# Moving the statistics of one norm, one tile of another, and the buffer of the recurrence's first input

## The chip, the core and the metric

The kernel runs on one core of a Trainium2 chip. A core has five engines that run their own instruction streams and wait for each other through semaphores: TensorE (PE in the profile, its weight loads PEld), VectorE (DVE), ScalarE (ACT), GpSimd (POOL) and SyncE (SP), which here issues nearly all DMAs. The metric is the device time of one execution in microseconds (us), as a median over runs.

## The reference, cut to what matters

Two layers act on 2 sequences of 1024 tokens with 512 channels. The kernel cuts the 2048 tokens into four blocks of 512 (b = 0 to 3).

```python
x = L0_attn_hidden_states
x = _layernorm(x + _L0_attn_ref(x, ...))   # mamba: in-projection, causal conv, scan, gate, RMS norm, out-projection
x = _layernorm(x + _L0_ffn_ref(x, ...))    # one linear layer, rows scaled by a tanh of their norm
x = _layernorm(x + _L1_attn_ref(x, ...))   # gated linear recurrence: conv, two gates, scan, out-projection
x = _layernorm(x + _L1_ffn_ref(x, ...))    # gated FFN of 512 -> 2048 -> 512 with integer weights

def _layernorm(x, axis=-1, eps=1e-05):
    m = jnp.mean(x, axis=axis, keepdims=True)
    v = jnp.var(x, axis=axis, keepdims=True)
    return (x - m) / jnp.sqrt(v + eps)
```

## The kernel before

**Who sets the order.** Python generators interleave the stages of neighbouring blocks: the order in which instructions are traced. A scheduler then orders each engine's stream by priority (earlier traced first) among what is ready in its own simulation. Three things bind it: `manual_schedule` for the opening, `high_priority` (not used at the places of this change before it), and `keep_in_program_order(ins)`, which pins an instruction behind the instruction of its engine that was traced just before it. That orders issue only; it is no wait for data.

**First layer, by block.** `project(b)` makes eight convolved channel tiles `inner(m)`: four matmuls `px` (L366), copies by ScalarE (L508, L336), three taps on VectorE (`causal_conv`, L292) and a SiLU (L342). Woven in are the decay products: ScalarE copies rows of `L` into PSUM (`pl`, L566), VectorE scans them (L572), GpSimd multiplies them (L587). `fill`, the generator `conclude(b - 1)`, puts the output projection of the block before (`po`, L764, and the residual update on VectorE, L779) between them, by `plan = (0, 0, 2, 0, 2, 0, 2, 2)`: eight steps, which are all the steps up to the last residual update. What follows in `conclude`, `layernorm(X[b])` and `store_rows(x_mid[b], X[b])`, is traced in the ninth step, which `weave` takes inside `recur(b)`, after the instructions of its first chunk of 128 tokens (`py` L691 and L699, `pst` L709, updates of the state L716 and L723, `by_token` L668 and L670).

**`layernorm`** (L274) makes per tile of 128 rows `bn_stats` (L279) and `bn_aggr` (L280) on VectorE, one square root on ScalarE (L282), one reciprocal (L283) and four scalings (L285) on VectorE or on the engine given.

**`head(b + 1)`** follows in the same alternation: for blocks 2 and 3 it turns the input with four VectorE transposes (`turn_blocks`, L270), each pinned; the first one is therefore queued behind the last scaling of the norm just traced. TensorE then makes `pbc` (L387) from it, from which the decays of the next block come.

**Second layer and recurrence.** `later_layers` weaves `conclude(3)` with `linear(0)` and `linear(1)`. Each `linear(b)` transposes its input on TensorE (`pt`, L237), splits it into two parts (`wu` by ScalarE L241, `wd` by VectorE L244), multiplies (`po`, L968), and ends with a norm whose four scalings run on GpSimd. Then `branches(0)` transposes X[0] (L237), ScalarE copies the result to `xT` (L248), and the products `p` (L1050) read it. `xT` of block 0 lies in pool `rp`, tag "xT"; that pool is on the right side, which the first layer's tiles used till then. The input of `linear(3)`, `mid`, lies in pool `wp`, tag "w4", and is loaded from `x_mid[3]`, which `conclude(3)` stores; the tag "w4" later takes the recurrence's output weights. In `rp`, tag "xT" serves `xT` of blocks 1 to 3 afterwards.

Of the kernel before, what the change touches and what calls it, by code (L numbers as in the profile page):

```python
# [9 lines left out]
F32 = mybir.dt.float32  # L10
# [6 lines left out]
P = 128  # L17
TB = 512
NJ = TB // P
D = 512  # L20
NK = D // P
# [16 lines left out]
def model_kernel(ctx: ExitStack, tc: tile.TileContext, t: dict, out: bass.AP):  # L38
    nc = tc.nc
# [6 lines left out]
    x_mid = tc.dram_tile([NBLK, TB, D], F32, name="x_mid")  # L46
# [35 lines left out]
    X = [tokens() for _ in range(3)]  # L82
# [140 lines left out]
        nc.vector.tensor_scalar(r, z, 0.0, None, ALU.max)  # L223
        nc.vector.scalar_tensor_tensor(o, p, 2.0, r, ALU.mult, ALU.add)

    def transposed(pool, b, X, tags=("xT",), split=False, bufs=1, by_act=False, behind=False):


        pieces = [
            pool.tile([P, NK, TB], F32R if split else F32, tag=tag, name=f"{tag}{b}", bufs=bufs)  # L230
            for tag in tags
        ]
        xT = pieces[0]
        for k in range(NK):
            pt = bank("pt")
            for j in range(NJ):
                nc.tensor.transpose(  # L237
                    pt[:, j * P : (j + 1) * P], X[b][:, j, k * P : (k + 1) * P], ident
                )
            if split:  # L240
                copied = nc.scalar.copy(xT[:, k, :], pt)  # L241
                if behind:
                    tc.keep_in_program_order(copied)
                nc.vector.tensor_tensor(  # L244
                    pieces[1][:, k, :], pt, xT[:, k, :].bitcast(F32), ALU.subtract
                )
            elif k % 2 or by_act:
                nc.scalar.copy(xT[:, k, :], pt)  # L248
            else:
                nc.vector.tensor_copy(xT[:, k, :], pt)  # L250
        return pieces
# [6 lines left out]
    def load_blocks(dst, rows, pinned=False):  # L258

        blocks = rows.rearrange("(n t) (k a c) -> a t k n c", t=32, k=NK, c=32)  # L260
        for a in range(4):
            load = nc.sync.dma_start(
                dst[32 * a : 32 * a + 32].rearrange("t k (n c) -> t k n c", c=32), blocks[a]
            )
            if pinned:
                tc.keep_in_program_order(load)
# [4 lines left out]
            if pinned:  # L271
                tc.keep_in_program_order(turned)

    def layernorm(x, n=NJ, engine=nc.vector):  # L274

        mv = sp.tile([P, NJ, 2], F32, tag="mv", name="mv")
        for j in range(n):
            st = sp.tile([P, 6], F32, tag="st", name="st", bufs=4)
            nc.vector.bn_stats(st, x[:, j, :])  # L279
            nc.vector.bn_aggr(mv[:, j, :], st)  # L280
        rs = sp.tile([P, NJ, 1], F32, tag="rs", name="rs")
        nc.scalar.activation(rs[:, :n], mv[:, :n, 1:2], AF.Sqrt, bias=eps)  # L282
        nc.vector.reciprocal(rs[:, :n], rs[:, :n])  # L283
        for j in range(n):
            engine.tensor_scalar(  # L285
                x[:, j, :], x[:, j, :], mv[:, j, 0:1], rs[:, j, :], ALU.subtract, ALU.mult
            )

# [467 lines left out]
    def conclude(b, st):  # L756


        xc, sums = st["xc"], st["sums"]
        rms = sp.tile([P, NJ], F32, tag="rms", name="rms")  # L760
        for j in range(NJ):
            po = bank("po")
            for m in range(NX):
                nc.tensor.matmul(  # L764
                    po, xc[:, m, j * P : (j + 1) * P], w_out[:, m, :],
                    start=(m == 0), stop=(m == NX - 1),
                )
                if m == NX // 2 - 1:
                    yield
            if j == 0:  # L770
                pss = bank("pss")
                for i in range(NJ):
                    nc.tensor.matmul(
                        pss[:, i : i + 1], sums[:, i * P : (i + 1) * P], ones,
                        start=True, stop=True,
                    )
                nc.scalar.activation(rms, pss[:, :NJ], AF.Sqrt, bias=eps, scale=1.0 / DI)
                nc.vector.reciprocal(rms, rms)
            nc.vector.scalar_tensor_tensor(  # L779
                X[b][:, j, :], po, rms[:, j : j + 1], X[b][:, j, :], ALU.mult, ALU.add  # L780
            )
            yield
        layernorm(X[b])
        store_rows(x_mid[b], X[b])

    def by_blocks(b, st):
# [4 lines left out]
    H, before, st = None, None, {}  # L791
# [10 lines left out]
    for b in range(NBLK):  # L802
# [19 lines left out]
        before, st = st, coming  # L822
    before_last.close()
    last = (conclude(NBLK - 1, before), first_layer.close)
# [41 lines left out]
    def later_layers(exact, last=None):  # L866


        suffix = "" if exact else "g"
        WT = F32R if exact else F32  # L870
        X = Y
# [4 lines left out]
        wp = opened.enter_context(tc.tile_pool(name="w" + suffix, bufs=1, reuse_waits="tile"))  # L876
# [72 lines left out]
        def linear(b):  # L949

            tags = ("wu0", "wd0") if exact else ("wu0",)
            if b == NBLK - 1:
                turn_blocks(mid)
                w1.append(wp.tile([P, NK, D], F32, tag="w4", name="w14" + suffix))
                xT = [ep.tile([P, NK, TB], WT, tag=tag, name=f"{tag}{b}") for tag in tags]
                split(mid, xT)
                nc.sync.dma_start(w1[4], w_sources["w_out"])
            else:

                xT = transposed(ep, b, X, tags=tags, split=exact, behind=b == 2)  # L960
            yield
            o = ep.tile([P, NJ, D], F32, tag="wF", name="o" + suffix)
            ssq = sp.tile([P, NJ], F32, tag="ssq", name="ssq")
            for j in range(NJ):
                po = bank("po")
                for k in range(NK):
                    for x in xT:
                        nc.tensor.matmul(  # L968
                            po, x[:, k, j * P : (j + 1) * P], wf[:, k, :],
                            start=(k == 0 and x is xT[0]), stop=(k == NK - 1 and x is xT[-1]),  # L970
                        )
                nc.vector.tensor_tensor(o[:, j, :], po, f0s, ALU.mult)
                junk = ep.tile([P, GW], mybir.dt.bfloat16, tag="junk", name="junk2")
                nc.scalar.activation(junk, o[:, j, :], AF.Square, accum_out=ssq[:, j : j + 1])
                if j % 2:
                    yield
            norm = sp.tile([P, NJ], F32, tag="norm", name="norm")
            nc.scalar.activation(norm, ssq, AF.Sqrt)
            v = sp.tile([P, NJ], F32, tag="v", name="v")
            nc.vector.tensor_scalar(v, norm, 1e-7, None, ALU.max)  # L980
            f = sp.tile([P, NJ], F32, tag="f", name="f")
            nc.scalar.activation(f, v, AF.Tanh)
            nc.vector.tensor_scalar(v, v, 1e-7, None, ALU.add)
            nc.vector.reciprocal(v, v)
            nc.vector.tensor_tensor(f, f, v, ALU.mult)
            nc.vector.tensor_tensor(norm, norm, f, ALU.mult)
            nc.vector.tensor_scalar(norm, norm, 1e-7, None, ALU.max)
            nc.vector.reciprocal(norm, norm)
            nc.vector.tensor_scalar(norm, norm, 0.99, 1.0, ALU.mult, ALU.min)
            nc.vector.tensor_tensor(f, f, norm, ALU.mult)  # L990
            for j in range(NJ):
                nc.vector.scalar_tensor_tensor(
                    X[b][:, j, :], o[:, j, :], f[:, j : j + 1], X[b][:, j, :],
                    ALU.mult, ALU.add,
                )
            layernorm(X[b], engine=nc.gpsimd)
            if b:
                store_rows(x_lin[b], X[b])
            yield
# [8 lines left out]
                pass  # L1008
        for i, name in ((2, "w_ig"), (3, "w_ag")):
            nc.sync.dma_start(w1[i], w_sources[name])  # L1010

        mid = wp.tile([P, NK, TB], F32, tag="w4", name="mid" + suffix)
        load_blocks(mid, x_mid[3])
        nc.sync.dma_start(X[3], rows_mid[3])

        def gate_up(m):

# [25 lines left out]
        with tc.tile_pool(name="rec" + suffix, bufs=1, side="right", reuse_waits="tile") as rp:  # L1043
            carry = rp.tile([P, NK, 3], F32, tag="carry", name="carry1")
            last_h = rp.tile([P, NK], F32, tag="last", name="last")

            def product(i, m, rhs):
                pm = bank("p1")
                for k in range(NK):
                    nc.tensor.matmul(  # L1050
                        pm, w1[i][:, k, m * P : (m + 1) * P], rhs[:, k, :],
                        start=(k == 0), stop=(k == NK - 1),
                    )
                return pm

            def branches(b, st):

                if b:
                    xT = rp.tile([P, NK, TB], F32, tag="xT", name=f"xT{b}")
                    turn_blocks(xT, lin.pop(0))  # L1060
                    if b + 1 < NBLK:
                        lin.append(coming_block(b + 1))
                else:
                    xT = transposed(rp, b, X, by_act=True)[0]
                yield
                cv = st["cv"] = rp.tile([P, NK, TB], F32, tag="cv", name="cv", bufs=2)
                y = st["y"] = rp.tile([P, NK, TB], F32, tag="y", name="y", bufs=2)
# [98 lines left out]
            st = {}  # L1166
# [260 lines left out]
```

## Time and profile before

| what | us |
|---|---|
| median of 3 runs (1121.63 to 1123.01) | 1121.71 |
| profiled execution, whole time | 1122.32 |
| its span, first to last instruction | 1120.5 |
| stretch of block 1's projection, from its third `px` pair to the first token transposes | 119.08 to 161.34 |
| the same stretch of block 2 | 226.49 to 264.33 |

The page gives busy time by engine, a row of busy tenths over 40 slices, the costliest groups and the chain of work that ended last. Further views are the waits of one engine (who was waited for, total us, how often, longest), the timeline of one engine (start, length, line, tile, count, and in brackets the idle time before it with what ended it), and tables of stretches (busy us and instructions of each engine, granted TensorE clock as a share of full speed, DMA share, GB/s). Times in all of them count from the start of the span.

### The profile page before, as it was taken

The numbers are of one execution on the slowest core, as the hardware profiler recorded it, in microseconds if no ns is written. First come the engines' busy times: TensorE is split into PE (matmuls) and PEld (weight loads), VectorE is DVE, ScalarE is ACT, GpSimd is POOL, SyncE is SP. The second block draws the span as 40 slices with busy tenths as digits, with TensorE's granted clock in tenths as the row PEclk, the third lists the DMA queues.
The fourth block names the chain that finished last, engine by engine and source line by source line (L and its number), as shares of the span: only waits on it lengthen the run. The fifth ranks groups of instructions, "written<-read, shape, count | busy, mean of one in ns | idle before, by whom it ended". The sixth has DMA issues, their size and how long they took to land.

```text
span 1120.5 us, 12075 instructions
## 1 busy us (share of the span) xinstructions
PE 1102.6 (98%) x4450; PEld 664.5 (59%) x4450; DVE 704.6 (63%) x1266; ACT 453.6 (40%) x692; POOL 366.5 (33%) x347
## 2 busy tenths in 40 slices
PE   9999999999999999999999999999999999999996
PEld 5455445445544555645444444447888888888885
DVE  5989897697869676874646438184238865325224
ACT  3334633463454233556644372553223224224223
POOL 1547471465248340453433231236411001001000
PEclk9999999999999999999999999999999999999999
DMA  9005302801220138246540001304654002100001
GB/s 325 19 11 119 95 1 92 206 1 38 82 105 0 39 125 224 57 103 151 112 76 8 30 1 38 38 0 130 193 100 75 1 1 59 17 1 29 9 1 41
DMA packets 122059, 77.04 MB, mean 69 GB/s; under 512 B 94512, under 2 KB 95312, under 8 KB 120456
## 3 DMA queue, kind: packets, MB, share of 16 engines
q1 hardware_dynamic: 120792, 75.77, 25.9%
q8 instruction: 37, 0.61, 0.2%
q10 hardware_dynamic: 976, 0.39, 0.1%
q14 instruction: 30, 0.25, 0.1%
q0 software_dynamic: 224, 0.02, 0.0%
HBM read 59.95 MB, written 16.02 MB: 68 GB/s over the span
## 4 chain that ended last, share of the span: by engine, by line
PE 82%; DVE 10%; ACT 4%; issue 1%; POOL 1%; DMA 1%; SPq 0%; DVEq 0%; ACTq 0%; POOLq 0%
PE pgu L1024 20%; PE p L1050 19%; PE po L1250 10%; PE pg L366 9%; PE px L366 7%; PE po L764 6%; PE po L1139 2%; PE py L699 2%; PE po L968 2%; DVE L L572 2%; DVE acc L292 2%; PE pxt L668 1%; POOL x L1145 1%; DVE st L279 1%; PE pbc L387 1%
## 5 line engine op out<-in xcount | busy, mean ns | idle before, releaser
L1035 DVE SCALAR_TENSOR_TENSOR h<-pgu,L_ffn_up_scale,sg 128x512 f32<-128x512 f32 x63 | 47.1, 748 | 126.5 <-PE pgu L1024 122.7
L764 PE MATMUL po<-w_out,xc 128*128 128x512 f32 x256 | 114.2, 600 | 2.2 <-DVE L L572 2.2
L366 PE MATMUL px<-xT,w_in 128*128 128x512 f32 x256 | 114.6, 597 | 0.0
L587 POOL TENSOR_TENSOR L<-L,gm 128x512 f32<-128x512 f32 x64 | 93.0, 1483 | 64.8 <-DVE bdec L582 38.3
L366 PE MATMUL pg<-xT,w_in 128*128 128x512 f32 x256 | 113.5, 594 | 0.0
L1050 PE MATMUL p<-xT,w 128*128 128x512 f32 x256 | 111.1, 592 | 1.0 <-ACT xT L248 1.0
L1050 PE MATMUL p<-cv,w 128*128 128x512 f32 x256 | 110.8, 592 | 0.0
L1024 PE MATMUL pgu<-wF__4239,wg 128*128 128x512 f32 x256 | 101.7, 397 | 0.0
L1024 PE MATMUL pgu<-lo__4240,wg 128*128 128x512 f32 x256 | 100.8, 394 | 0.0
L1024 PE MATMUL pgu<-lo__4240,wu 128*128 128x512 f32 x256 | 100.7, 393 | 0.0
L1024 PE MATMUL pgu<-wF__4239,wu 128*128 128x512 f32 x256 | 100.7, 393 | 0.0
L1250 PE MATMUL po<-wd,hh 128*128 128x512 f32 x252 | 98.3, 396 | 0.3 <-POOL wg L911 0.3
L1250 PE MATMUL po<-wd,hl 128*128 128x512 f32 x252 | 98.2, 396 | 0.2 <-DVE hl L1039 0.2
L1034 ACT ACTIVATE sg<-pgu,L_ffn_gate_scale 128x512 f32<-128x512 f32 x63 | 43.4, 689 | 125.6 <-PE pgu L1024 125.5
L764 PEld LDWEIGHTS po<-w_out,xc 128*128 128x128 f32 x256 | 49.0, 192 | 64.3 <-issue 57.1
L1038 ACT CAST hh<-h 128x512 fp32r<-128x512 f32 x63 | 39.1, 621 | 114.6 <-DVE h L1035 114.4
L1050 PEld LDWEIGHTS p<-xT,w 128*128 128x128 f32 x256 | 48.5, 190 | 60.8 <-issue 57.6
L1050 PEld LDWEIGHTS p<-cv,w 128*128 128x128 f32 x256 | 48.6, 190 | 60.4 <-issue 59.1
L366 PEld LDWEIGHTS px<-xT,w_in 128*128 128x128 f32 x256 | 47.5, 190 | 57.5 <-issue 56.2
L366 PEld LDWEIGHTS pg<-xT,w_in 128*128 128x128 f32 x256 | 47.3, 190 | 54.2 <-issue 53.3
L292 DVE SCALAR_TENSOR_TENSOR acc<-xpad,cols,acc 128x512 f32<-128x512 f32 x72 | 67.2, 935 | 18.9 <-ACT acc L336 14.1
L1368 POOL TENSOR_TENSOR x<-x,r 128x512 f32<-128x512 f32 x12 | 15.2, 1300 | 194.2 <-DVE r L1367 194.2
(291 smaller groups left out, 1929.2 us busy)
## 6 DMA issues: line engine op xcount, KB each, us to landing
L<-decays SPq DMA_DIRECT2D x12, 1024.0 KB, 7.1
x_mid<-x SPq DMA_DIRECT2D x4, 1024.0 KB, 4.3
x<-x_mid SPq DMA_DIRECT2D x4, 1024.0 KB, 8.1
st<-in_L_ffn_gate_w_dram SPq DMA_DIRECT2D x8, 512.0 KB
st<-in_L_ffn_up_w_dram SPq DMA_DIRECT2D x8, 512.0 KB, 3.9
st<-in_L_ffn_down_w_dram SPq DMA_DIRECT2D x8, 512.0 KB, 4.1
x_rec<-x SPq DMA_DIRECT2D x4, 1024.0 KB, 4.7
x<-_attn_hidden_states_dram SPq DMA_DIRECT2D x3, 1024.0 KB
```

The source lines that it names most:

```text
L292: tap = nc.vector.scalar_tensor_tensor(acc, xpad[:, k : k + TB], w[:, k : k + 1], acc, ALU.mult, ALU.add)
L366: nc.tensor.matmul(pm[:n, :], w_in[:, k, lo : lo + n], xT[:, k, :], start=(k == 0), stop=(k == NK - 1),)
L572: nc.vector.tensor_tensor_scan(L[:, h, :], pl, id4.rearrange("p j t -> p (j t)"), 0.0, ALU.mult, ALU.add)
L587: nc.gpsimd.tensor_tensor(L[:, h, :], L[:, h, :], st["gm"], ALU.mult)
L699: nc.tensor.matmul(pys[i][hh * HD : (hh + 1) * HD, q, :], dtx[q][:, 2 * i + hh, :], L[:, h, s], start=(first and q == 0), stop=(q == 1), s ...
L764: nc.tensor.matmul(po, xc[:, m, j * P : (j + 1) * P], w_out[:, m, :], start=(m == 0), stop=(m == NX - 1),)
L1024: nc.tensor.matmul(pm, w[g][:, k, cols], x[:, k, :], start=(k == 0 and x is pieces[0]), stop=(k == NK - 1 and x is pieces[-1]),)
L1034: nc.scalar.activation(sg, pgu[0], AF.Silu, scale=gs[:, m : m + 1])
L1035: nc.vector.scalar_tensor_tensor(h, pgu[1], us[:, m : m + 1], sg, ALU.mult, ALU.mult)
L1038: nc.scalar.copy(halves[0], h)
L1050: nc.tensor.matmul(pm, w1[i][:, k, m * P : (m + 1) * P], rhs[:, k, :], start=(k == 0), stop=(k == NK - 1),)
L1250: nc.tensor.matmul(po[j], x[:, j * P : (j + 1) * P], wd[m // GK][:, m % GK, :], start=(m == 0 and x is h[0]), stop=(m == NF - 1 and x is h ...
```

## The change

Four edits:

- The norm in `conclude(0)` pins each `bn_stats` behind the VectorE instruction traced before it. For the first it is the last product of `by_token` in the first chunk of `recur(1)`; for the others the `bn_aggr` of the tile before.
- In `linear(0)`'s norm the fourth scaling runs on VectorE, the other three stay on GpSimd.
- `xT` of block 0 goes to pool `wp`, tag "w4", and its four ScalarE copies get high priority.
- `mid` goes to pool `rp`, tag "xT"; its four loads and the load of X[3] are traced after that pool is opened.

```diff
-    def transposed(pool, b, X, tags=("xT",), split=False, bufs=1, by_act=False, behind=False):
+    def transposed(pool, b, X, tags=("xT",), split=False, bufs=1, by_act=False, behind=False, soon=False):
...
+            elif soon:
+                with tc.high_priority():
+                    nc.scalar.copy(xT[:, k, :], pt)
             elif k % 2 or by_act:
                 nc.scalar.copy(xT[:, k, :], pt)
...
-    def layernorm(x, n=NJ, engine=nc.vector):
+    def layernorm(x, n=NJ, engine=nc.vector, last=None, pinned=False):
...
-            nc.vector.bn_stats(st, x[:, j, :])
+            stats = nc.vector.bn_stats(st, x[:, j, :])
+            if pinned:
+                tc.keep_in_program_order(stats)
             nc.vector.bn_aggr(mv[:, j, :], st)
...
-            engine.tensor_scalar(
+            (last if last and j == n - 1 else engine).tensor_scalar(
                 x[:, j, :], x[:, j, :], mv[:, j, 0:1], rs[:, j, :], ALU.subtract, ALU.mult
             )
...
-        layernorm(X[b])
+        layernorm(X[b], pinned=b == 0)
         store_rows(x_mid[b], X[b])
...
-            layernorm(X[b], engine=nc.gpsimd)
+            layernorm(X[b], engine=nc.gpsimd, last=None if b else nc.vector)
...
-        mid = wp.tile([P, NK, TB], F32, tag="w4", name="mid" + suffix)
-        load_blocks(mid, x_mid[3])
-        nc.sync.dma_start(X[3], rows_mid[3])
...
+            mid = rp.tile([P, NK, TB], F32, tag="xT", name="mid" + suffix)
+            load_blocks(mid, x_mid[3])
+            nc.sync.dma_start(X[3], rows_mid[3])
...
-                    xT = transposed(rp, b, X, by_act=True)[0]
+                    xT = transposed(wp, b, X, tags=("w4",), by_act=True, soon=True)[0]
```

## The prediction

> **What bounds the kernel now.** First the page's busy row and the waits of TensorE, by quarters of the span.
>
> ```profile
> PE 1102.6 (98%) x4450; PEld 664.5 (59%) x4450; DVE 704.6 (63%) x1266; ACT 453.6 (40%) x692; POOL 366.5 (33%) x347
> PE po L764 <- DVE L L572: 2.2, 2, 1.9
> PE p L1050 <- ACT xT L248: 1.0, 1, 1.0
> PE pt L237 <- POOL xpad L1072: 0.4, 1, 0.4
> ```
>
> TensorE bounds the kernel. It is idle for 17.9 us in all; about 8.4 of that is the tail, about 2 the start. So an edit pays only where it closes a hole of TensorE or shortens its matmuls. The three waits shown are the holes beside which the four edits lie. From 464 us to the FFN's end the stretches show TensorE busy throughout but for 0.5 us, so time won before it arrives at the end.
>
> Next the table of stretches (columns: busy us and count of PE, PEld, DVE, ACT, POOL; clock; DMA share; GB/s), block 1 above block 2:
>
> ```profile
> 133.39:142.37 8.98, 7.03 (x17) 2.85 (x15) 8.88 (x14) 6.11 (x12) 8.32 (x8) 1.00 0.00 0
> 142.37:151.04 8.67, 8.67 (x17) 3.74 (x17) 8.64 (x11) 1.62 (x3) 7.07 (x5) 0.80 0.00 0
> ...
> 240.30:247.17 6.87, 6.87 (x18) 3.04 (x16) 6.84 (x11) 5.97 (x11) 5.85 (x7) 1.00 0.00 0
> 247.17:254.03 6.86, 6.86 (x17) 3.04 (x16) 6.86 (x10) 1.34 (x3) 6.54 (x7) 1.00 0.00 0
> ```
>
> Sixteen matmuls take 6.87 us in block 2. In block 1 the first sixteen are followed by a hole of 1.95, and the next sixteen take 8.67 at a mean clock of 0.80: the two-us windows show the clock at 0.50 from 144 to 146. The whole stretch is 42.26 us (119.08 to 161.34) against 37.84 (226.49 to 264.33) for the same matmuls: 4.42 us are to be had at most.
>
> What VectorE does ahead of the hole:
>
> ```profile
> 136.47 0.70 DVE L279 BATCH_NORM_STATS2 st<-x 128x6 f32<-128x512 f32 x1
> 137.21 0.18 DVE L280 BATCH_NORM_AGGREGATE mv<-st 128x2 f32<-128x6 f32 x1
> 137.31 0.72 DVE L779 SCALAR_TENSOR_TENSOR x<-po,rms,x 128x512 f32<-128x512 f32 x1
> 138.06 0.69 DVE L279 BATCH_NORM_STATS2 st<-x 128x6 f32<-128x512 f32 x1
> 138.79 0.18 DVE L280 BATCH_NORM_AGGREGATE mv<-st 128x2 f32<-128x6 f32 x1
> 138.88 4.55 DVE L572 TENSOR_TENSOR_SCAN L<-pl,id 128x512 f32<-128x512 f32 x4
> 142.37 8.83 PE L764 MATMUL po<-w_out,xc 128*128 128x512 f32 x16 [1.95 <-DVE L L572]
> ```
>
> Two pairs of statistics stand before the scans whose end frees TensorE. In block 2 only one pair stands there, and TensorE does not wait.
>
> **Statistics: what goes.** The pin puts all four pairs behind the first chunk of `recur(1)`. Before the scans that frees 0.82 + 0.85 (the chain's pieces) = 1.67 us. The scans can't use all of it: ScalarE's copies `pl` start at 136.80 and take 0.53 each, so the first scan can start at 137.37 instead of 138.88: 1.51. The hole shrinks from 1.95 to 0.44. What is late next is VectorE. Its sixth convolution ends at 152.2 instead of 153.7. The seventh then waits for ScalarE's SiLU and two copies; block 2 shows 1.93 between the same two convolutions (258.37 to 260.30), so it starts at 154.1 instead of 156.10 and, at its own 4.3, ends at 158.4. Before, VectorE then idled 1.15 for `po`; TensorE, at 119.08 + 37.84 + 0.23 + 0.44 = 157.6, is now there first. The residual update (0.67) follows at once, and the token products (L670) start at 159.1 to 159.3 instead of 162.21. Gain 3.0; bounds 1.5 (the hole alone) and 4.4 (the stretch of block 2).
>
> [...] The row shows half clock behind a hole of only 1.95, and none behind 1.03 at 463. [...] By the row they go with the hole: 3.0. I take the row.
>
> **Statistics: what comes.** Behind 159.3 VectorE keeps its work without the pair at 163.4 and ends the second chunk's token products near 166 (before 169.37, with that pair, the reciprocal and one scaling among them). Then four pairs of 0.85 (3.4), the root (0.4 with its hand-over), the reciprocal (0.2) and four scalings (1.92 in block 2): 171.8. The transposes of block 2's input are pinned behind the last scaling:
>
> ```profile
> 169.29 1.45 DVE L285 TENSOR_SCALAR x<-x,mv,rs 128x512 f32<-128x512 f32 x3
> 170.65 2.48 DVE L270 STREAM_TRANSPOSE xT<-xT 128x512 f32<-128x512 f32 x4
> 177.37 1.51 DVE L292 SCALAR_TENSOR_TENSOR acc<-rpad,cwr,acc 32x512 f32<-32x512 f32 x2 [4.24 <-ACT acc L336]
> ```
>
> They run 171.8 to 174.3, while TensorE, 3.0 earlier, is ready for `pbc` at 170.7. `pbc` would wait; but the scheduler takes the next ready instruction, and the second chunk's `py`, `pst`, `pxt` (4.1 us) are ready by then. I cost this at nothing, with them as cover; without the cover it is rival B. What hangs on `pbc` has room: the decay rows are issued at 192.92 and their loads at 199.30, the first scan of block 2 comes at 225.72. VectorE's 4.24 idle at 177 takes up the rest. The store of `x_mid[0]` moves with the norm on SP's queue; the reload is at 411.
>
> **Second place: `xT`, `mid`, one tile.** ScalarE's, GpSimd's and SP's timelines:
>
> ```profile
> 463.27 2.05 ACT L248 COPY xT<-pt 128x512 f32<-128x512 f32 x4 [0.48 <-DMA x_mid<-x]
> ...
> 451.02 8.42 POOL L285 TENSOR_SCALAR x<-x,mv,rs 128x512 f32<-128x512 f32 x4 [32.70 <-PE pt L237]
> ...
> 458.89 0.37 SPq L254 DMA_DIRECT2D x_mid<-x  x1
> ```
>
> The copies wait for the store of X[3], because `xT` takes the place of a tile that this store reads. In "w4" nothing of that kind stands; the transposes start at 458.6, ScalarE is free, and high priority puts the copies (0.59) ahead of the squares. TensorE's 1.03 goes. `mid` needs that store anyway, as its data; its loads stay behind it on SP (two at 463.21, two at 482.06 behind the store of `x_lin`), and VectorE turns it at 494.87. The next `xT` then waits for `mid`'s last reader (500.2) instead of the products at 498.8, but is turned only at 529.50. The output weights, now behind `xT`, were issued at 518.18 and used at 589. All covered.
>
> The 0.42 is the wait for the fourth tile on GpSimd (2.1 us a tile, end 459.44; the wait row names the memset right behind it). With it on VectorE the third ends at 457.3 and the hole goes. VectorE pays one scaling: 0.54 alone, 0.68 beside GpSimd at 455.50, 1.51 at worst (a row at 756). If it lands before `wd` (L244, 451.34), for which TensorE already waits 0.15 at 452.07, up to 0.6 comes back. [...] By the row at 455.50 it is slowed by 0.14. I take the row. This place: 0.85 to 1.45, taken as 1.2.
>
> **Sum.** 3.0 + 1.2 = 4.2. From the profiled 1122.32 (span 1120.5 and 1.8 around it) to 1118.1; that execution lies 0.6 above the median, so from 1121.71 to **1117.5**, with its own range 1116.0 to 1119.0. A measurement of this kernel can tell 0.2% (2.2 us) from no change.
>
> **Rivals.** *B, the wait moves.* `pbc` keeps its place in TensorE's order and waits for the late transposes: it ends at 174.8 instead of 172.6, 2.2 lost, 1119.7. For: in all blocks `pbc` stands behind two gate tiles. Against: the scheduler sees VectorE's queue. *C, slower.* The same wait, decided by the root: if ScalarE has it behind the second gate tile's SiLU (170.7 + 0.6, a table load of 1.28, 0.3), scalings and transposes end at 177.5 and `pbc` at 178.0: 5.4 lost, and a hole of that size brings the half clock, 1.8 more. 7.2 against 4.2: 1124.7. It decides once the wait at `pbc` exceeds 2.4 (with the clock). Against: in blocks 1 and 2 the root stands before the gates' SiLU (164.34, 270.74). *D, the change does not do what it says.* Another early-ready VectorE instruction takes the freed place before the scans, or a bank is late, and 0.5 is won in block 1: with 1.2, 1120.0.
>
> **Chances.** Forecast 0.57, B 0.16, C 0.15, D 0.12. Faster takes the forecast and half of B: 0.65; same the other half and D: 0.20; slower C: 0.15. The range runs from 1115.7 (4.42 + 1.6) to 1122.5, which holds the forecast, B and D and leaves C out.
>
> **What would show it.** Right: no `bn_stats` between 120 and 163, the stretch near 39 us, clock 1.00 in it, the waits of `po` on L572 below 0.7, `p` not waiting on `xT`. Wrong: a wait of `pbc` on L270, a dip of the clock near 171, a longer wait of `po` L968 on `wd`, or decay loads of block 2 landing late.

## The result, and the profile after

| | median, us | range | executions |
|---|---|---|---|
| before | 1121.81 | 1120.89 to 1123.49 | 22 |
| changed | 1124.39 | 1121.33 to 1125.01 | 22 |

The ratio is 1.0014, with a 95% interval of 1.0008 to 1.002: 0.14% slower where 0.37% faster was forecast. (The two medians alone give 1.0023; they depend on how many executions of each group below they hold.) That is less than the 0.2% which the prediction had set as the bound of a change, and the median lies outside its range of 1115.7 to 1122.5.

The times of the changed kernel fall into groups: five executions lie between 1121.33 and 1121.66, fourteen between 1124.29 and 1125.01, three between them. Those of before do the same: twelve between 1120.89 and 1121.90, ten between 1122.84 and 1123.49. The profiled execution of the changed kernel (1121.35, span 1119.5) is one of its lower five; that of before (1122.32) had the half clock (0.50) in 144 to 146. Two further profiles of the changed kernel caught its upper group (1124.85 and 1124.70); the first of them, with a span of 1123.1, is shown. Both groups are needed to see where the time went.

First the page's busy row and the waits of TensorE in the changed kernel (columns as before: total us, how often, longest).

```profile
PE 1100.4 (98%) x4450; PEld 663.8 (59%) x4450; DVE 704.2 (63%) x1267; ACT 452.7 (40%) x692; POOL 364.2 (33%) x346
...
PE pbc L393 <- issue: 2.0, 1, 2.0
PE po L770 <- DVE L L578: 1.3, 2, 0.8
PE po L974 <- DVE wd L244: 0.8, 1, 0.8
```

The old waits are gone or smaller: `po` on the scans (now L578) is at 1.3 instead of 2.2, and neither the wait on `xT` nor the one on GpSimd is left. Two have come: `pbc` for 2.0, and `po` on `wd` at 0.8 instead of 0.15. (A third, `pt` on the load of the first input, 1.0 near 7 us, differs between profiles of one kernel, and the stretch of block 1 begins within 0.2 us of before in all of them.) The row names "issue" for `pbc`, a wait for nothing that the profile shows. The timelines tell what it was. TensorE, changed kernel:

```profile
127.08 7.13 PE L770 MATMUL po<-w_out,xc 128*128 128x512 f32 x16 [0.83 <-DVE L L578]
...
141.58 7.13 PE L770 MATMUL po<-w_out,xc 128*128 128x512 f32 x16 [0.49 <-DVE L L578]
...
164.35 7.03 PE L372 MATMUL pg<-xT,w_in 128*128 128x512 f32 x16
173.41 0.64 PE L393 MATMUL pbc<-xT,w_bc 128*48 128x256 f32 x4 [2.02 <-issue]
173.97 0.48 PE L697 MATMUL py<-cdec,H 32*128 32x128 f32 x2
174.39 0.64 PE L393 MATMUL pbc<-xT,w_bc 128*48 128x256 f32 x4
174.96 0.48 PE L697 MATMUL py<-cdec,H 32*128 32x128 f32 x2
175.37 1.07 PE L393 MATMUL pbc<-xT,w_bc 128*48 128x256 f32 x8
```

VectorE, changed kernel, the last two rows ahead of `pbc`:

```profile
170.77 1.91 DVE L291 TENSOR_SCALAR x<-x,mv,rs 128x512 f32<-128x512 f32 x4
172.60 2.48 DVE L273 STREAM_TRANSPOSE xT<-xT 128x512 f32<-128x512 f32 x4
```

The hole at which the pin was aimed is nearly closed, 0.49 for 1.95. The one before the scans ahead of it is 0.83, for 0.23 in before. That is no work of the change: another profile of the changed kernel (the one of its second run, below) has 0.49 and 0.23 there.

```profile
PE po L770 <- DVE L L578: 0.7, 2, 0.5
```

So executions of one kernel differ by 0.6 at this place, and the two profiles compared here happen to differ in it; why is not shown. Further on, TensorE stands still from 171.4 and starts `pbc` when the first of the four transposes is done; the products come in three pieces, with a few `py` of the next chunk between them. From the start of the gate tiles `pg` to the second group of the next chunk's `py` (those that read `L`) the time is 12.66 us (164.35 to 177.01); before it was 9.49 (166.72 to 176.21). 3.17 us are given back here.

The starts of the same instructions in three profiles, and the difference from before:

| start of | before | changed, lower group | changed, upper group |
|---|---|---|---|
| first token transposes `pxt`, block 1 | 161.34 | 158.85 (-2.49) | 158.98 (-2.36) |
| gate tiles `pg` behind the first chunk | 166.72 | 164.35 (-2.37) | 164.48 (-2.24) |
| `py` (with `L`) of the second chunk | 176.21 | 177.01 (+0.80) | 179.60 (+3.39) |
| gate tiles behind the second chunk | 179.61 | 180.41 (+0.80) | 183.64 (+4.03) |
| first transposes of `linear(0)` | 449.08 | 449.87 (+0.79) | 453.10 (+4.02) |
| `p` about 29 us later | 478.64 | 477.70 (-0.94) | 480.91 (+2.27) |
| end of the span | 1120.5 | 1119.5 (-1.0) | 1123.1 (+2.6) |

Three things happen, each at one place: 2.4 won ahead of 164, 3.2 or 6.3 lost between 164 and 184, 1.7 won between 450 and 478. The two groups of the changed kernel part at the second of them: of the 3.6 us between their spans 3.1 arise there, 0.1 ahead of it and 0.4 behind 481. The stretches of TensorE in the upper group (length, busy us and count, granted clock, DMA share, GB/s):

```profile
172.00:174.00 2.00, 0.47 (x4) 1.00 0.13 48
174.00:176.00 2.00, 2.00 (x9) 0.53 1.02 383
176.00:178.00 2.00, 2.00 (x10) 0.50 0.25 93
178.00:180.00 2.00, 2.00 (x20) 0.50 0.00 0
180.00:182.00 2.00, 2.00 (x32) 0.76 0.42 45
```

Behind the hole the clock is at half until about 181; in the profile of the lower group all these rows show 1.00. That costs 3.1 us (gate tiles at 183.64 instead of 180.41, of which 0.13 was there at 164).

### The profile page after: what moved, and what is told of

It is laid out like the page before. It is cut to its first block, busy times and chain, and to the rows that moved or that the text cites. A ratio compares the mean times of both kernels' runs of the same rounds, so it can differ in the third digit from the quotient of the medians.

```text
span 1119.5 us, 12077 instructions
## 1 busy us (share of the span) xinstructions
PE 1100.4 (98%) x4450; PEld 663.8 (59%) x4450; DVE 704.2 (63%) x1267; ACT 452.7 (40%) x692; POOL 364.2 (33%) x346
## 4 chain that ended last, share of the span: by engine, by line
PE 81%; DVE 11%; ACT 4%; issue 2%; POOL 1%; DMA 1%; SPq 0%; DVEq 0%; ACTq 0%; POOLq 0%
PE pgu L1026 20%; PE p L1056 19%; PE po L1257 10%; PE pg L372 9%; PE px L372 7%; PE po L770 4%; DVE acc L298 3%; PE po L1146 2%; PE py L705 2%; PE po L974 2%; DVE L L578 2%; PE pxt L674 1%; PE py L697 1%; PE pt L237 1%; POOL x L1152 1%
## 5 line engine op out<-in xcount | busy, mean ns | idle before, releaser
L1040 ACT CAST hh<-h 128x512 fp32r<-128x512 f32 x63 | 39.1, 620 | 114.6 <-DVE h L1037 114.4
L1056 PE MATMUL p<-xT,w 128*128 128x512 f32 x192 | 82.9, 592 | 0.0
L578 DVE TENSOR_TENSOR_SCAN L<-pl,id 128x512 f32<-128x512 f32 x64 | 75.0, 1205 | 4.7 <-ACT pl L572 2.5
```

The lines of the kernel that those rows point to most:

```text
L578: nc.vector.tensor_tensor_scan(L[:, h, :], pl, id4.rearrange("p j t -> p (j t)"), 0.0, ALU.mult, ALU.add)
L1040: nc.scalar.copy(halves[0], h)
L1056: nc.tensor.matmul(pm, w1[i][:, k, m * P : (m + 1) * P], rhs[:, k, :], start=(k == 0), stop=(k == NK - 1),)
```

## The experiments

The theory was: the pinned statistics win ahead of the first chunk what was forecast, and lose it at `pbc`, with the half clock on top in most executions; the second place works as forecast. The rivals were that the second place loses (the wait on `wd`), and that the rest of the loss comes from elsewhere, such as the store moved on SP. Every ratio below is against before, run on the same chip.

**The changed kernel once more**, without an edit.

> The changed kernel once more. Theory 1 (the wait moved: the late statistics delay the transposed input of block 2, TensorE waits about 2 us before pbc, its narrow matmuls there come in pieces, and in most executions the clock halves behind that): times in two groups, near 1121.4 and near 1124.5, median near 1124.4; where the profiled execution is of the upper group, its clock dips between 170 and 185 us. Rival theory 2 (the second place, xT and mid, costs the time, for instance through the interleaving of linear layers and products): the dip or the lost time lies behind 450 us.

Measured: 1122.09 (1120.77 to 1125.09, 14 executions), ratio 1.0008 (0.9999 to 1.0018). Seven lie in the lower group, six in the upper, one between. The lower group was 5 of 22 in the first measurement and is 7 of 14 here, so the median moved by 2.3 us with nothing changed. The profiled execution is of the lower group; in it the token transposes start at 158.39. The two of the upper group both have the dip of the clock between 174 and 182 (0.50 in their rows of 176 to 180).

**Only the pin, and everything but the pin.** The first is before with the statistics pinned:

```diff
-        layernorm(X[b])
+        layernorm(X[b], pinned=b == 0)
```

> The kernel before with the pinned statistics alone. Theory 1: the second place won 1.7 us and the statistics lost the rest, so this is 1.7 slower than the changed kernel: 1126.0 (1125 to 1127), slower than before by 0.4%. Theory 2: this keeps the forecast gain of 3.0, so near 1119.

Measured: 1126.31 (1122.48 to 1126.45, 5), ratio 1.0038 (1.0025 to 1.0051). The second is the changed kernel with that line set back:

> The changed kernel without the pin: xT in w4, mid in rp, one scaling on VectorE. Theory 1: 1.7 faster than before, 1120.1 (1119.5 to 1120.8), still in two groups 1.8 apart, since the hole before the scans stays. Theory 2: near 1124 or slower.

Measured: 1120.05 (1119.15 to 1121.95, 15), ratio 0.9981 (0.9973 to 0.9989). Medians mix the groups here too, so like is compared with like, on this one chip:

| median of | lower group | upper group |
|---|---|---|
| before | 1121.46 (15 executions) | 1123.15 (13) |
| pin alone | 1122.48 (1) | 1126.38 (4) |
| changed | 1121.32 (7) | 1124.70 (6) |
| all but the pin | 1119.71 (11) | 1121.15 (4) |

(The granted clock over the span is 0.997 or 0.998 in the lower groups and 0.994 to 0.996 in the upper, but for one execution of before at 0.997; the one changed execution between its groups is left out.) The pin alone loses 1.0 and 3.2, though its lower group is a single execution. The second place wins 1.8 and 2.0 without the pin, and 1.2 and 1.7 with it. So the rival that the second place loses falls. Without the pin the groups lie 1.4 apart, for 1.8 forecast.

**The whole norm behind the chain's consumer.** In the changed kernel the norm of block 0 with its store leaves `conclude` and is traced behind the first step of `head(2)`, so that the input's transposes come before it on VectorE:

```diff
-        layernorm(X[b], pinned=b == 0)
-        store_rows(x_mid[b], X[b])
+        if b:
+            layernorm(X[b])
+            store_rows(x_mid[b], X[b])
...
+    def norm_behind(ahead):
+        yield next(ahead)
+        layernorm(X[0], pinned=True)
+        store_rows(x_mid[0], X[0])
+        yield from ahead
...
+                if b == 1:
+                    ahead = norm_behind(ahead)
```

> The changed kernel with the norm of block 0 traced behind the first step of block 2's head, so that the four transposes come ahead of the statistics. Theory 1: the wait before pbc (3.2 us with its pieces) and the clock dip behind it go, the gain before the scans stays: 1118.2 (1117.5 to 1119.0), in one group. Theory 2: no gain over the changed kernel, near 1124.

Measured: 1118.28 (1117.82 to 1118.69, 5), ratio 0.9966 (0.9953 to 0.9979). The five executions lie within 0.9 us: one group. TensorE in this kernel:

```profile
164.40 7.03 PE L372 MATMUL pg<-xT,w_in 128*128 128x512 f32 x16
171.36 1.93 PE L393 MATMUL pbc<-xT,w_bc 128*48 128x256 f32 x16
173.22 0.73 PE L697 MATMUL py<-cdec,H 32*128 32x128 f32 x16
```

And VectorE:

```profile
166.96 2.47 DVE L273 STREAM_TRANSPOSE xT<-xT 128x512 f32<-128x512 f32 x4
...
180.98 0.68 DVE L283 BATCH_NORM_STATS2 st<-x 128x6 f32<-128x512 f32 x1
```

Up to 164.4 it is the changed kernel. Then the transposes run at 166.96 instead of 172.60, `pbc` follows the gate tiles with no wait and in one piece, and the statistics start at 180.98, where nothing is late for them. Their store moves on SP's queue from 172.71 to 188.16, later still than in the changed kernel, and costs nothing: that rival falls too. From the gate tiles to the second chunk's `py` (173.88) it takes 9.48 again. That names the place of the loss and shows that the gain ahead of it can be kept.

**The same norm without the second place**, that is, before with that edit alone.

> The kernel before with only the norm of block 0 behind the transposes of block 2, no edit at the second place. Theory 1: the second place is worth 1.7 everywhere, so 1118.3 + 1.7 = 1120.0 (1119.5 to 1120.6), in one group; the statistics' own gain is then 1.9 against the median of before, and 1.4 against its lower group. Rival (the two places interact): off that by more than 0.6.

Measured: 1119.97 (1119.24 to 1120.56, 21), ratio 0.9981 (0.9974 to 0.9987). The statistics, put well, are worth 1.8 against the median of before: 1.6 against its lower group on this chip (19 executions, median 1121.54) and 3.0 against its upper (12, median 1122.99). The second place adds 1.7 (1119.97 to 1118.28). The two places add up.

**A longer hole.** Every pinned `bn_stats` of the changed kernel is issued twice, with the same result, so that VectorE is later by four of them:

```diff
-            stats = nc.vector.bn_stats(st, x[:, j, :])
+            for again in range(2 if pinned else 1):
+                stats = nc.vector.bn_stats(st, x[:, j, :])
```

> The changed kernel with each of the four pinned statistics of block 0 taken twice. Theory 1: the transposes come 2.6 us later, the wait before pbc grows from 2.0 to about 4.6, the half clock follows in every execution: 1127 (1126.5 to 1128), one group, and the profile shows the clock dip between 172 and 185 us. Rival (the dip has another place or cause): no dip there, 1124 with the old two groups shifted by 2.6.

Measured: 1126.82 (1126.38 to 1127.37, 4), ratio 1.0048 (1.0033 to 1.0064). TensorE:

```profile
176.60 3.65 PE L394 MATMUL pbc<-xT,w_bc 128*48 128x256 f32 x16 [5.13 <-issue]
```

The hole is 5.13 instead of 2.02, longer by 3.11, and VectorE's transposes start at 175.79 instead of 172.60, later by 3.19: the wait that the profile calls "issue" follows VectorE's chain. The four executions lie within 1 us, all with a granted clock of 0.993 to 0.995, and the profiled one has the half clock (0.50 from 174 to 180); `pbc` takes 3.65 in one piece instead of 1.93. It is also the plainest sign that TensorE's order does not bend: with 5 us to fill, `pbc` still stands ahead of `py`.

**`pbc` later in TensorE's order.** If the order doesn't bend by itself, it can be traced so: `head(2)` is put one step later, which sets the second chunk's `py`, `pst`, `pxt` and two gate tiles ahead of `pbc`, the cover that the prediction had counted on.

```diff
+    def one_chunk_later(ahead):
+        yield
+        yield from ahead
...
+                if b == 1:
+                    ahead = one_chunk_later(ahead)
```

> The changed kernel with block 2's head traced one chunk later, the statistics still pinned where the change puts them: TensorE's order has the second chunk's py, pst, pxt and two gate tiles ahead of pbc. Theory 1 (the cover of the forecast works once the order gives it): no wait before pbc, near e4_norm_late, 1118.3 (1117.6 to 1119.0). Rival (the chain behind pbc has no room): the token factors or the decays of block 2 come late and it is 1120 or more.

Measured: 1124.51 (1124.03 to 1125.53, 9), ratio 1.0024 (1.0014 to 1.0034). A miss for the theory: the cover works (no wait before `pbc`, and block 2's `px` at 224.14 instead of 226.49 of before), and 6 us are lost later. The `py` run at 171.34, so they were ready all through the hole of the changed kernel (171.4 to 173.4), and only the order kept them out. SP's queue and TensorE in this kernel:

```profile
201.95 0.50 SPq L494 DMA_DIRECT2D decays<-work  x1
...
203.93 0.39 SPq L602 DMA_DIRECT2D L<-decays  x1
204.96 8.59 SPq L265 DMA_DIRECT2D xT<-_attn_hidden_states_dram  x4
213.59 2.70 SPq L602 DMA_DIRECT2D L<-decays  x3
```

```profile
171.34 0.73 PE L697 MATMUL py<-cdec,H 32*128 32x128 f32 x16
...
182.36 1.93 PE L393 MATMUL pbc<-xT,w_bc 128*48 128x256 f32 x16
...
244.21 3.70 PE L372 MATMUL px<-xT,w_in 128*128 128x512 f32 x8 [2.66 <-DVE L L578]
249.88 7.13 PE L770 MATMUL po<-w_out,xc 128*128 128x512 f32 x16 [1.96 <-DVE L L578]
```

`pbc` is at 182.36, 9 us later than before, and the decay rows are written at 201.95 instead of 192.92. Then only one of the four loads of `L` gets ahead of the next block's input on SP (three in before), and three wait 9 us behind it. The scans that need them are late, and TensorE waits 2.66 and 1.96 for them. In the changed kernel `pbc` ends 0.8 later than in before and the decay rows are written at 194.26, 1.3 later, without such a wait. So that much room is there, and not 9 us; where between the two it ends was not tried.

**The parts of the second place**, on the kernel with the norm behind the transposes. First with all four scalings on GpSimd, as before the change:

```diff
-            layernorm(X[b], engine=nc.gpsimd, last=None if b else nc.vector)
+            layernorm(X[b], engine=nc.gpsimd)
```

> As e4_norm_late, but with all four scalings of the second layer's first norm on GpSimd again. Theory 1: the scaling on VectorE closed the wait of 0.42 for the fourth tile and opened one of 0.64 before wd, so undoing it wins 0.2: 1118.1 (1117.7 to 1118.5). Rival (the tile is what the second place gains from): 0.4 or more slower than e4_norm_late.

Measured: 1118.25 (1117.65 to 1118.53, 7), ratio 0.9969 (0.9957 to 0.998). TensorE in this kernel:

```profile
449.06 0.50 PE L984 MATMUL po<-wfr,wd 128*128 128x512 f32 x1 [0.15 <-DVE wd L244]
...
456.47 3.39 PE L237 MATMUL pt<-ident,x 128*128 128x128 f32 x29 [0.43 <-POOL xpad L1089]
```

The tile on VectorE takes away the 0.43 and makes 0.15 into 0.79: a draw. From the first transposes of `linear(0)` to the `p` of the table above it takes 27.81 us here and 27.79 with the tile on VectorE (29.54 without the second place). The move of the one tile is worth nothing, and the 1.7 come from the exchange of the two buffers with the priority of the copies. Then, from that kernel, without the priority:

```diff
-                with tc.high_priority():
-                    nc.scalar.copy(xT[:, k, :], pt)
+                nc.scalar.copy(xT[:, k, :], pt)
```

> As e5_late_four_pool, with xT in w4 but its four ScalarE copies without high priority; ScalarE's order then has the squares and the norm's root between them. Theory 1 (the place alone frees the copies, the priority puts them ahead of about 2 us of other work): the products wait again by 0.5 to 1.5, 1119.2 (1118.7 to 1119.8). Rival (the store was the only thing the copies waited for): 1118.2, no change.

Measured: 1117.91 (1117.82 to 1118.2, 5), ratio 0.9966 (0.9952 to 0.998). A second miss: ScalarE now does squares between the copies, the first copy starts at 457.17 and the last at 460.83, and the time does not rise. The stretch just named is 28.12, 0.3 more than with the priority, but the spans of the two profiles are equal (1116.0). So the exchange of the buffers brings nearly all of the gain: what held the copies was the store in the way of their buffer.

The three kernels with the late norm and the exchanged buffers (1118.28, 1118.25, 1117.91) beat both the kernel before and the changed one; the last does without the tile on VectorE and without the priority, and moves the whole norm instead of its statistics.

## Why the prediction was wrong

**The step that failed** is "I cost this at nothing, with them as cover": the second chunk's `py`, `pst` and `pxt` were to fill TensorE while `pbc` waits for the late transposes. I had asked what is ready, and not whether anything would move. TensorE stood still instead: the place cost 3.17 us at full clock and 6.27 with the half clock. TensorE's stream in the changed kernel keeps the order of before but for four `py` let in between the pieces of `pbc`, and with 5.13 us of hole it keeps it still. The price of this step was there, as rival B; its chance, 0.16, was the mistake. B itself was priced at 2.2; it came to 3.17, since the transposes ended at 175.1 instead of the 174.3 worked out, and `pbc` came in pieces behind them until 176.4.

**The clock was charged on one side only.** I took the row (half clock behind a hole of 1.95), let the slow matmuls go with the hole, and booked the clock as gain. Rival B made a hole of the same length and was priced without a clock; C asked for more than 2.4. The row was right on both sides: the hole of 2.02 brings the half clock in most executions (20 of 36 lie in the upper group, and both profiles of that group show it), 3.1 us each. The outcome is B with the clock of C.

**The gain of 3.0 was right for the execution it was read from, and not for the median.** The profiled execution of before contains the half clock. Ten of its 22 executions lie in its upper group, some 1.7 above the lower, so the median does not contain it as a whole. In the trace the token transposes came 2.49 earlier, and 2.95 earlier in the profile of the changed kernel's second run, which like that of before has only 0.23 at the earlier scans. With the norm where it costs nothing the gain is 3.0 against the upper group of before, 1.6 against the lower, and 1.8 against the median. "That execution lies 0.6 above the median, so from 1121.71" shifted the start and kept the gain, and that can't be done when the gain is that very difference.

**What held.** The hole before the scans is 0.49, for 0.44 forecast; the stretch of block 1's projection is 39.7 us (119.14 to 158.85), and 39.1 in the profile of the second run (119.28 to 158.39), for "near 39"; the clock in it is 1.00. No `bn_stats` stands ahead of the first chunk, VectorE's chain behind it came out within 1 us, and the root did not wait behind the SiLU.

**The second place** was sized at 1.2 and gave 1.7. The two holes closed as forecast, and 0.6 came back at `wd`, as feared: 1.45 - 0.64 = 0.81 of idle time. The rest, 0.92, is not idle time at all: it was in rows that count as busy (below). The moved scaling took 0.71 beside GpSimd's tiles (451.81 to 458.00), for 0.68 in the row at 455.50 that the prediction took:

```profile
452.13 0.71 DVE L291 TENSOR_SCALAR x<-x,mv,rs 128x512 f32<-128x512 f32 x1
```

That 0.7, ahead of `wd` on VectorE, was paid by TensorE, as the row of `wd` had warned.

**What hangs on `pbc`** "has room": true for the change, where the decay rows came 1.3 later and no wait of block 2 says otherwise. With 9 us it is wrong, because the loads fall behind others in SP's queue.

Nothing here tells why the scheduler took four `py` and no more. The experiments show that it did not refill the hole, not by what rule.

## What to carry to other kernels

When work is pinned later, follow its last instruction to whoever is queued behind it, and look where that consumer stands in the stream of the engine that sets the time: the order of these kernels, made ahead of time, did not bend round a late operand, with holes of 2.02 and 5.13 to fill. Move the whole group behind the consumer, or leave it. And when a short hole (1.95 here) shows half clock in one trace, count the clock with every hole of that length, the new one too, and take the gain from the distribution of times and not from the one execution that was profiled.

## What the runs showed of the hardware

**The half clock comes in some executions of a kernel and not in others.** It came behind holes of 1.95 and 2.02 in a part of the executions: 10 of 22 (before), 14 of 22 and 6 of 14 (changed), counted by the groups of times. With 5.13 all four have a granted clock of 0.993 to 0.995, and in the profiled one it set in within the hole (0.92 in 172 to 174, 0.50 in 174 to 176). It did not come behind 2.66 and 1.96 in the profile of the kernel with `pbc` later (1.00 in 240 to 260), nor behind 1.03 at `xT` in that of before (1.00 from 462 to 472). With the late norm alone, which leaves the second place as in before, the granted clock over the span is 0.997 or 0.998 in all 21 executions.

The length of the half clock is an estimate from the granted clock in rows of two us: 3.4 us in before and in all but the pin, 6.8, twice that, in both profiles of the changed kernel's upper group and with the statistics taken twice. By the same rows it began some 0.6 us behind the hole in one of the two profiles of the upper group, and some 1.5 behind the same hole in the other. The three executions between the groups of the changed kernel lie some 1.6 above the lower one, which is what 3.4 us of half clock cost before; none of them was profiled. The half clock cost some 1.7 us before and 3.1 in the changed kernel, where `pbc` in pieces and `py` on 32 rows follow the hole; why it lasts twice as long there is not shown. The granted clock over the whole span (in the changed kernel 0.998 in the lower group, 0.994 or 0.995 in the upper) tells the groups apart without a trace.

**A wait can be inside busy time.** In before, TensorE's weight loads of `linear(1)`, 6 us behind the hole at `xT` (start, us, in brackets the idle time before):

```profile
470.42 0.19 PEld L968 LDWEIGHTS po<-wfr,wd 128*128 128x128 f32 x1 [0.60 <-DVE wd L244]
...
471.08 0.19 PEld L968 LDWEIGHTS po<-wfr,wd 128*128 128x128 f32 x1 [0.37 <-DVE wd L244]
...
471.68 0.19 PEld L968 LDWEIGHTS po<-wfr,wd 128*128 128x128 f32 x1 [0.30 <-DVE wd L244]
```

Each load waits for a tile of VectorE, while the matmul rows beside them follow without a gap: six matmuls take 1.84 us (470.42 to 472.26) where the next six take 1.39. ScalarE starts on `wu` at 465.19, behind the late copies of `xT`, and VectorE on these tiles, `wd`, at 469.70, behind four statistics. From the first `p` to the compared one it took 14.73 us with no idle time; in the changed kernel it takes 14.19 (463.51 to 477.70), where `wu` starts at 463.29, `wd` at 463.93, and these loads are not late. Another 0.38 is in the transposes ahead, whose rows a hole had cut in two. A busy row of 98% was thus no bound for what this place could give.
